# Channel stage: the outer column groups of the Toeplitz tile loaded over 48 of each 64 partitions, on SyncE's queue

## The chip, the cores and the metric

The kernel runs on one core of one Trainium2 chip. The metric is the device time of one execution in microseconds (us), the median of several runs. The time before is 10363.48 us, the median of 3 runs from 10363.17 to 10363.57.

## The reference

Four layers follow each other on an image tensor x of shape (32, 192, 56, 56), each a residual on a group-normalized input (32 groups of 6 channels):

```
x = x + agent_attention(_gn(x))            # layer 0
x = x + bidirectional_wkv_scan(_gn(x))     # layer 1
x = x + shift_and_3x3(_gn(x), offset)      # layer 2
x = x + long_conv(_gn(x), z, W1, W2, W3)   # layer 3
```

Layer 2 moves each channel by its own whole number of rows and columns and applies a separable 3 x 3 kernel of its own. Layer 3 makes a 55 x 55 filter for each channel out of a small network and convolves each 56 x 56 image with it, so that the output row j takes the input rows j-27 to j+27:

```
def _L3_conv_ref(x, z, W1, ..., deltas, shift, bias, distance_map):
...
    xf = jnp.fft.rfft2(x, s)
    kf = jnp.fft.rfft2(k[0], s)
    y = jnp.fft.irfft2(xf * kf[None], s)
    y = y[..., Kh // 2:Kh // 2 + H, Kw // 2:Kw // 2 + W]
    return y + bias * x
```

Layers 2 and 3 work within a channel (and the group of 6 channels for the normalization); the kernel runs them together in its last stage, the channel stage.

## The kernel before, in words

Everything is float32. The program first makes the filters and writes, for every channel, a table `spans` to HBM: for each channel 7 column groups of 128 rows of 84 numbers (42 frequencies, cosine and sine). Then come the attention stage (layer 0), the scan stage (layer 1), which writes its result to HBM as `x2` with a channel's 32 images together, and from about 8243 us to the end the channel stage, `channel_blocks` (L1550). The change touches only this stage.

The channel stage works on one channel at a time, with all 32 images in one tile: the 128 partitions are two halves of 64 (even and odd images), 56 of them image rows. The loop at its end runs c from -1 to 204 and treats three channels in each turn, 6 or 12 channels apart, so that a group of 6 is finished before its mean and spread are needed. In iteration c:

- `load(c + 3)` issues two DMAs on SyncE's queue (SP in the profile), one for each half: 56 rows of 3584 bytes from `x2` into one of ten `x` tiles.
- `norm(c + 2)` normalizes on GpSimd (POOL) with two operations on 128 x 896 (tile `xn`). Every fourth channel, `find_matrices` makes the next shift matrices there.
- `move_rows(c + 1)` shifts and filters along the rows: 8 matmuls into two PSUM banks, two copies on ScalarE (ACT) into `across`.
- `analyse(c - 11)` transforms a centred channel along one axis: matmuls against a table (`ps<-fixed,padded` in the profile), 12 copies on ACT into `y`.
- `move_columns(c)` is the second half of layer 2 (`ps<-cols,across`), added to `x` on VectorE (DVE).
- `synthesise(c - 13)` and `finish` (`ps<-z,fixed`): the inverse transform, added on DVE into `done`, and two DMAs to the output on SP's queue, each of 896 pieces of 224 bytes.
- `convolve(c - 12)`: for each of 42 frequencies a matmul of the spectra `y` with a slice of the Toeplitz tile (`ps<-toep,y`), the product over all input rows at once. ACT moves the result to `turned` in three steps; DVE transposes it for the next turn.
- `load_toeplitz(c - 9)` (L1655 to L1663) loads the Toeplitz tile for the channel that is three turns ahead, into the one of three `toep` tiles that this turn's `convolve` has just read. This is one DMA of 2352 KB on ACT's queue.

The matmuls stand in the program in the order rows, analysis, columns, synthesis, convolution, and on every engine the order of the program is kept (`_InOrder`, L1538), queue issues included. Where instructions of different engines meet, semaphores are put in by the framework. For DMAs of both hardware queues it has eight semaphores, handed out in turn in the order in which its scheduler lists the DMAs; each DMA issue therefore waits until the one handed out eight places earlier has landed.

A `toep` tile is 128 partitions by 56 output rows by 84 numbers. The 128 partitions are the cosine and sine parts of 64 input rows each (56 in use, in reversed order). The 56 output rows are 7 column groups of 8 (`SPAN`); partition p of group q holds 8 consecutive rows, 2688 bytes, that start at row p of the group's 128 rows in `spans`. Rows beyond the reach of the filter are zeros in the table. All constant tiles are cleared once at the stage's start (L1589 to L1596).

Of the kernel before, what the change touches and what calls it, by code (L numbers as in the profile page):

```python
# [30 lines left out]
S = 56  # L31
# [37 lines left out]
HALF = 64  # L69
FREQ = 2 * NF  # L70
LAGS = 2 * S
SPAN = 8
# [1477 lines left out]
def channel_blocks(ctx: ExitStack, tc: tile.TileContext, taps, k, x2, rs2, spans, out):  # L1550
# [8 lines left out]
    nc = tc.nc  # L1559
# [7 lines left out]
    pe, vector, scalar, pool, sync = (_InOrder(tc, e) for e in (nc.tensor, nc.vector, nc.scalar, nc.gpsimd, nc.sync))  # L1567
# [6 lines left out]
    pieces, at = [], 0  # L1574
    for rows, shape in CHANNEL:
        n = int(np.prod(shape))
# [6 lines left out]
    def kept(name, shape, n):  # L1583
        return [cp.tile(shape, F32, name=f"{name}{i}", tag=f"{name}{i}") for i in range(n)]

    xs, padded = kept("x", [128, NI, S], 10), kept("padded", [128, NI, HALF], 8)
    toep, turned = kept("toep", [128, S, FREQ], 3), kept("turned", [128, S, 32], 2)
    across = kept("across", [2 * S, NG, 2, HALF], 2)
    for t in across:  # L1589
        nc.vector.memset(t[:, :, :, S:HALF], 0.0)  # L1590
    for t in xs:
# [63 lines left out]
    def load_toeplitz(c):  # L1655

        if not 0 <= c < C:
            return
        t = toep[c % len(toep)].rearrange("p j f -> p (j f)")
        n = S // SPAN  # L1660
        first = spans[c * n * 128]
        there = bass.AP(first.tensor, first.offset, [[FREQ, 128], [128 * FREQ, n], [1, SPAN * FREQ]])
        scalar.dma_start(out=t.rearrange("p (q f) -> p q f", q=n), in_=there)  # L1663

    def move_rows(c):

# [136 lines left out]
    for c in range(3):  # L1803
        load(c)
        load_toeplitz(c)
        if c < 2:
            norm(c)
    rows, spectra = {}, {}

    def within(c):  # L1810
        return 0 <= c < C

    for c in range(-1, C + LATE + 1):
        m, b, e = c - GROUP, c - LATE, c - LATE - 1
        q = groups[m // GROUP] if within(m) and m % GROUP == 0 else None
# [29 lines left out]
        if within(b):  # L1845
            convolve(b, spectra.pop(b))
            load_toeplitz(b + 3)
# [23 lines left out]
@with_exitstack  # L1871
def all_blocks(ctx: ExitStack, tc: tile.TileContext, a, k, out):
    nc = tc.nc
    NB = out.shape[0]
    dp = ctx.enter_context(tc.tile_pool(name="dram", bufs=1, space=DRAM))

    def scratch(name, shape):
        return dp.tile(shape, F32, name=name, tag=name)

    x1, x2 = scratch("x1", [NB, C, N]), scratch("x2", [C, 2, S, NB // 2, S])  # L1880
    filt, rs2 = scratch("filt", [C, KS * KS]), scratch("rs2", [C, 2, 2, NB // 2])
    lags, taps = scratch("lags", [C, 2, LAGS, FREQ]), scratch("taps", [128, C // 4, 12])
    spans = scratch("spans", [C * (S // SPAN) * 128 + SPAN, FREQ])
    st_a, st_c = scratch("st_a", [128, 2, NB // 2, 9]), scratch("st_c", [2, 64, 2, NB // 2, 9])
    with tc.tile_pool(name="a_r", bufs=1) as rp, tc.tile_pool(name="a_x", bufs=2) as xp:
        ready = _Ready(rp, xp)
        make_filter(tc, a, k, filt, lags, spans, taps, lambda: ready.load(nc, a, k))
        attention(tc, a, ready, x1, st_a, st_c, lambda b: copy_spans(tc, lags, spans, b))
    with tc.tile_pool(name="count", bufs=1) as cp:
        count = cp.tile([1, 1], I32, name="count", tag="count")  # L1890
        scan_pairs(tc, a, k, x1, st_a, st_c, x2, rs2, count)
        n = nc.values_load(count[0:1, 0:1], min_val=0, max_val=128)
        with tc.If(n > 0):
            scan_guarded(tc, a, k, x1, x2, rs2)
    channel_blocks(tc, taps, k, x2, rs2, spans, out)
# [109 lines left out]
```

## Time and profile before

| what | value |
|---|---|
| median of 3 runs | 10363.48 us |
| the profiled execution's own time | 10372.07 us |
| its span (first to last instruction) | 10370.2 us |
| mean granted TensorE clock | 0.962 |
| busy over the whole span: PE / DVE / ACT / POOL | 91% / 88% / 61% / 21% |
| start of the channel stage (first toep load issued) | 8242.9 us |
| first and last convolution matmul | 8348.6 and 10356.6 us |
| toep load: number, size, queue | 192 of 2352.0 KB, ACT |
| x load, channel stage: number, size, queue | 384 of 196.0 KB, SP |
| output store: number, size, queue | 384 of 196.0 KB, SP |

PE, PEld, DVE, ACT, POOL and SP are TensorE's matmuls, its weight loads, VectorE, ScalarE, GpSimd and SyncE; a q behind a name means the queue that issues (ACTq, SPq). L1546 is the helper that records every instruction of the channel stage, so these are told apart by their tiles, written out<-in. A bracket behind a row is the time the engine stood idle before it and what ended that. The granted clock is given as a share of full speed. The share of DMA is the mean over the core's 16 DMA engines and can pass 1 a little, since packets overlap.

### The profile page before, as it was taken

What the parts mean: (1) busy time and instruction counts of PE and PEld (TensorE: products, weight loads), DVE (VectorE), ACT (ScalarE), POOL (GpSimd) and SP (SyncE); (2) the same over time, 40 slices, a digit from 0 to 9 for tenths busy, and PEclk for the clock granted to TensorE, in tenths of its full rate; (3) what the DMA queues carried; (4) which work ended last, traced back from release to release, by engine and by line L of the source; (5) the groups of instructions that cost most, each with busy time, mean ns of one, the idle gap of its engine ahead of it and who ended that gap; (6) DMA issues with size and microseconds to landing.
All of it is one profiled execution on the core that took longest, in us unless ns stands there. A gap on an engine that the chain in (4) does not pass through costs nothing. (4 is left out here: it accounts for less than half of the span.)

```text
span 10370.2 us, 162899 instructions
## 1 busy us (share of the span) xinstructions
PE 9436.8 (91%) x63814; PEld 5816.8 (56%) x63814; DVE 9099.9 (88%) x11284; ACT 6324.4 (61%) x11964; POOL 2223.2 (21%) x1751
## 2 busy tenths in 40 slices
PE   5999999999999999998888888888888799999998
PEld 3555555655565555555333343333334488888886
DVE  5888888888888888887999999999999788888887
ACT  3555555555555555554566666666666567777777
POOL 0000000000000000000333333333333354554442
PEclk9999999999999999998899999999999899999999
DMA  4212221122112211111244444344444489999999
GB/s 129 68 37 66 68 68 44 58 68 68 47 55 68 68 46 29 49 49 43 69 107 101 103 103 105 104 104 101 101 101 101 129 247 303 307 306 304 304 304 278
DMA packets 1111096, 1247.61 MB, mean 120 GB/s; under 512 B 773091, under 2 KB 813440, under 8 KB 1098232
## 3 DMA queue, kind: packets, MB, share of 16 engines
q1 hardware_dynamic: 914284, 746.65, 28.1%
q10 hardware_dynamic: 196036, 490.46, 13.9%
q8 instruction: 506, 8.29, 0.3%
q14 instruction: 270, 2.21, 0.1%
HBM read 916.15 MB, written 306.43 MB: 118 GB/s over the span
## 5 line engine op out<-in xcount | busy, mean ns | idle before, releaser
L649 DVE SCALAR_TENSOR_TENSOR o<-v_a,att_w,o 128x896 f32<-128x896 f32 (+1 forms) x1024 | 1056.8, 1032 | 422.2 <-ACT v_a L623 301.9
L1167 POOL MEMSET f<- 128x2 f32 x48 | 4.5, 99 | 4751.2 <-DMA st_c<-st 4748.8
L1546 DVE STREAM_TRANSPOSE z<-turned 128x1792 f32<-128x1792 f32 x192 | 680.3, 3543 | 211.2 <-ACT turned L1546 211.2
L1546 ACT COPY y<-ps 64x252 f32<-64x252 f32 (+1 forms) x2304 | 784.6, 341 | 89.6 <-PE ps L1546 59.8
L1161 ACT ACTIVATE pq<-pq 128x784 f32<-128x784 f32 x384 | 329.4, 858 | 676.6 <-DVE pq L1157 676.4
L1153 DVE TENSOR_TENSOR_SCAN pq<-decay,f,both 128x784 f32<-128x784 f32 x384 | 695.7, 1841 | 9.1 <-ACT both L1183 9.1
L1157 DVE SCALAR_TENSOR_TENSOR pq<-both,eu,pq 128x1568 f32<-128x1568 f32 x384 | 701.3, 1840 | 2.0 <-POOL f L1156 0.4
L666 ACT ACTIVATE pr<-ps,low 98x896 f32<-98x896 f32 (+1 forms) x384 | 352.3, 918 | 572.7 <-DVE low L664 572.7
L1153 DVE TENSOR_TENSOR_SCAN pq<-decay,b,both 128x784 f32<-128x784 f32 x384 | 694.1, 1839 | 0.0
L921 PE MATMUL ps<-x,weights 128*128 128x392 f32 x1536 | 584.6, 519 | 83.4 <-ACT x L1141 54.2
L649 DVE SCALAR_TENSOR_TENSOR o<-v_c,att_w,o 128x448 f32<-128x448 f32 (+1 forms) x1024 | 638.6, 624 | 4.9
L662 PE MATMUL ps<-xs_a,gk_a 128*98 128x448 f32 (+1 forms) x1536 | 636.8, 495 | 0.0
L776 ACT ACTIVATE pq<-pq 128x1176 f32<-128x1176 f32 (+2 forms) x224 | 241.9, 1080 | 642.5 <-DVE pq L768 620.5
L663 PE MATMUL ps<-xs_c,gk_c 125*98 125x448 f32 (+1 forms) x1536 | 631.3, 492 | 0.0
L1141 ACT ACTIVATE x<-x,nb,rs 128x784 f32<-128x784 f32 x384 | 386.5, 1030 | 337.3 <-DMA x<-x 183.2
L1546 PEld LDWEIGHTS ps<-toep,y 128*32 128x32 f32 x16896 | 500.4, 151 | 160.9 <-issue 76.0
L763 PE MATMUL ps<-gq_a,xs_a 128*128 128x294 f32 (+1 forms) x1600 | 547.0, 425 | 37.7 <-DVE pq L768 33.1
L1546 PE MATMUL ps<-toep,y 128*32 128x112 f32 x16896 | 560.5, 286 | 12.6 <-DVE done L1546 11.1
L1156 POOL COPY b<-pq 128x2 f32<-128x2 f32 x192 | 394.7, 2056 | 660.9 <-DVE pq L1153 567.3
L1546 POOL TENSOR_TENSOR xn<-x,scale 128x896 f32<-128x896 f32 x192 | 329.7, 1717 | 937.4 <-DMA x<-x 670.5
L764 PE MATMUL ps<-gq_c,xs_c 125*128 125x294 f32 (+1 forms) x1600 | 519.9, 413 | 0.0
L1546 ACT ACTIVATE turned<-ps,rs 128x448 f32<-128x448 f32 (+1 forms) x576 | 377.3, 663 | 223.3 <-PE ps L1546 216.0
(360 smaller groups left out, 23488.2 us busy)
## 6 DMA issues: line engine op xcount, KB each, us to landing
toep<-spans ACTq DMA_DIRECT2D x192, 2352.0 KB
x<-x SPq DMA_DIRECT2D x576, 392.0 KB
x<-x SPq DMA_DIRECT2D x896, 196.0 KB
out_x<-done SPq DMA_DIRECT2D x384, 196.0 KB
spans<-lags SPq DMA_DIRECT2D x24, 2352.0 KB
x<-in_x SPq DMA_DIRECT2D x32, 1568.0 KB
x<-x SPq DMA_DIRECT2D x32, 1568.0 KB
gq_c<-once SPq DMA_DIRECT2D x32, 821.1 KB
```

The lines of the kernel that those rows point to most:

```text
L649: nc.vector.scalar_tensor_tensor(dst, tap(i), dww[:, t, i : i + 1], dst, ALU.mult, ALU.add)
L662: mm(ps[P2, h, :n], g[:, cols], xs_a[j][:, px], start=True, stop=False)
L663: mm(ps[P2, h, :n], gk_c[0:KC, 2 * j + h, cols], xs_c[j][0:KC, px], start=False, stop=True)
L666: nc.scalar.activation(pr[:, :, :n], ps[P2, :, :n], AF.Exp, bias=low[:, j, p : p + 1], accum_out=sums[:, j, p : p + 1])
L763: mm(ps[:m, k - q, :HA], xs_a[j][:, px], g, start=True, stop=False)
L764: mm(ps[:m, k - q, :HA], xs_c[j][0:KC, px], gq_c[0:KC, which[k]], start=False, stop=True)
L921: mm(out, aa, srcs[t][h], start=True, stop=False)
L1141: nc.scalar.activation(xs[t], xs[t], AF.Identity, bias=nb1[:, t, s.p : s.p + 1], scale=rs1[:, t, s.p : s.p + 1])
L1153: nc.vector.tensor_tensor_scan(to, decay[:, of(t)].to_broadcast([128, MC]), data, at[:, i : i + 1], ALU.mult, ALU.add)
L1156: nc.gpsimd.tensor_copy(at, z[:, :, last])
L1157: nc.vector.scalar_tensor_tensor(before, both, eu[:, of(t)], before, ALU.mult, ALU.add)
L1546: return lambda *args, **kw: self.tc.keep_in_program_order(do(*args, **kw))
```

## The change

The seven column groups are no longer loaded by one DMA. The middle three (groups 2 to 4) are loaded as before on ACT's queue, now 1008 KB. The outer four are loaded in pairs (groups 0 and 1, groups 5 and 6) by four DMAs on SP's queue, one for each pair and each 64-partition half: 48 partitions of 5376 bytes, 252 KB each. For groups 0 and 1 these are partitions 8 to 55 of the half, read from group 1's rows in `spans`; for groups 5 and 6 partitions 0 to 47, read from group 5's. The 16 partitions of each half that are left out are cleared at the stage's start, by 18 memsets on DVE (for three tiles, two halves and three ranges, 32 partitions by 1344 numbers each). Nothing of the arithmetic changes.

```diff
     across = kept("across", [2 * S, NG, 2, HALF], 2)
+    EDGE = 8
+    for t in toep:
+        for p in (0, HALF):
+            nc.vector.memset(t[p : p + 32, 0 : 2 * SPAN], 0.0)
+            nc.vector.memset(t[p + 32 : p + 64, 0 : 2 * SPAN], 0.0)
+            nc.vector.memset(t[p + 32 : p + 64, 5 * SPAN :], 0.0)
     for t in across:
         nc.vector.memset(t[:, :, :, S:HALF], 0.0)
...
         first = spans[c * n * 128]
-        there = bass.AP(first.tensor, first.offset, [[FREQ, 128], [128 * FREQ, n], [1, SPAN * FREQ]])
-        scalar.dma_start(out=t.rearrange("p (q f) -> p q f", q=n), in_=there)
+        there = bass.AP(
+            first.tensor, first.offset + 2 * 128 * FREQ, [[FREQ, 128], [128 * FREQ, 3], [1, SPAN * FREQ]]
+        )
+        scalar.dma_start(out=t.rearrange("p (q f) -> p q f", q=n)[:, 2:5], in_=there)
+        for q, p, to in ((1, EDGE, 0), (5, 0, 5)):
+            for m in range(2):
+                there = bass.AP(
+                    first.tensor, first.offset + (q * 128 + m * HALF) * FREQ, [[FREQ, S - EDGE], [1, 2 * SPAN * FREQ]]
+                )
+                at = HALF * m + p
+                sync.dma_start(out=t[at : at + S - EDGE, to * SPAN * FREQ : (to + 2) * SPAN * FREQ], in_=there)
```

## The prediction, made before the changed kernel ran

> **What bounds the kernel now.** I read the slices of the span first, then the windows of the channel stage, the list of waits, the DMA queues, and one iteration of the timeline.
>
> ```profile
> PE   5999999999999999998888888888888799999998
> DMA  4212221122112211111244444344444489999999
> ```
>
> From about 8350 us on, PE and the DMA engines are both full. The windows and the queues say how full (columns: time, then each engine's busy time, granted clock, DMA share, GB/s):
>
> ```profile
> 8600.00:10000.00 1400.00, 1375.54 (x19248) 1168.30 (x19248) 1222.22 (x1229) 1064.97 (x2413) 691.26 (x594) 1.00 1.02 304
> ```
>
> ```profile
> q10 hardware_dynamic: 17102, 45.19, 65.1%
> q1 hardware_dynamic: 36831, 15.11, 35.3%
> ```
>
> PE is busy for 98% and DMA for 102% (in the window from 9000 to 9200, 65.1% is ACT's queue, q10: the Toeplitz loads). Which of them is the limit is told by who waits for whom in the same 1400 us:
>
> ```profile
> POOL xn L1546 <- DMA x<-x: 476.9, 84, 13.7
> ...
> ACT turned L1546 <- PE ps L1546: 142.5, 207, 2.0
> ```
>
> No row has PE waiting for a DMA. Only POOL waits for one, the x loads, and one iteration shows why that is free:
>
> ```profile
> 9306.29 1.82 PE L1546 MATMUL ps<-rows,xn 128*112 128x112 f32 x16
> 9306.46 0.37 ACTq L1546 DMA_DIRECT2D toep<-spans  x1
> ...
> 9307.95 2.46 PE L1546 MATMUL ps<-fixed,padded 128*128 128x168 f32 x16
> ...
> 9310.25 1.94 PE L1546 MATMUL ps<-cols,across 112*128 112x112 f32 x16
> ...
> 9312.11 1.73 PE L1546 MATMUL ps<-z,fixed 128*64 128x448 f32 x8
> ...
> 9313.77 2.87 PE L1546 MATMUL ps<-toep,y 128*32 128x112 f32 x88
> ...
> 9315.86 1.69 POOL L1546 TENSOR_TENSOR xn<-x,scale 128x896 f32<-128x896 f32 x1 [7.33 <-DMA x<-x]
> 9316.03 2.52 SPq L1546 DMA_DIRECT2D x<-x  x2
> 9316.57 1.82 PE L1546 MATMUL ps<-rows,xn 128*112 128x112 f32 x16
> ...
> 9317.63 1.69 POOL L1546 TENSOR_TENSOR xn<-xn,scale 128x896 f32<-128x896 f32 x1
> ```
>
> PE runs rows, analysis, columns, synthesis, convolution back to back and starts again after 10.28 us. The xn finished at 9319.3 is read by the rows that start at about 9326.8: 7.5 us in hand. The toep load at 9306.46 is for the convolution three turns later. By the starts of the convolutions in the timeline the common period is 10.26 us; the mean of the 167 periods between 8475.6 and 10247.0 is 10.607, since every sixth turn has the group's mean and spread (11.3 to 12.8) and some lose 0.3 to 1.5 to DVE. So PE sets the pace, with 0.35 us a turn lost on top.
>
> **The change, part by part.**
>
> *Bytes.* Toeplitz falls from 2352 to 1008 + 4 x 252 = 2016 KB, 14%. By the queue's row that is 0.14 x 65.1 = 9 points of DMA share, 1.02 to 0.93. PE never waits for it, so it is worth nothing directly; at most the DVE losses shrink (see the rival).
>
> [...]
>
> *Memsets.* 18 of 32 x 1344. The rows beside them are 128x128 at 165 ns and 128x560 at 525 ns, 0.83 ns an element, so 1.18 us each and 21 us on DVE.
>
> ```profile
> 8244.72 1.12 DVE L1596 MEMSET turned<- 128x560 f32 x2
> ...
> 8270.37 0.62 DVE L1546 TENSOR_TENSOR x<-x,ps 128x448 f32<-128x448 f32 x1 [24.54 <-PE ps L1546]
> ```
>
> DVE's idle 24.5 us hides them; without that cover they would cost 21. The first pieces on SP wait for them, with the x of channels 1 to 3 queued behind. Bounds 0 and 8 us (three pieces of queue), taken: 2.
>
> *Moved to SP, and the semaphores.* This decides. A turn had five DMAs; now it has nine: x, x, out, out, four pieces on SP, and the middle load on ACT. With eight semaphores in turn, every issue waits for the landing of the DMA eight places earlier in the built order. I read that order in the changed program: before, the issue that waits for a Toeplitz load was mostly an output store, two turns after that load. After, the second x half of channel c+3 (which the loop issues at the start of iteration c) waits for the middle load of channel c-9, which ACT issues at the *end* of iteration c. So x(20) waits for toep(8), x(21) for toep(9), for every x from channel 18 to 191. In one iteration of six it is the first half, in one the last piece that stands ahead of both halves. Queued behind it on SP: the next stores, the four pieces, the next first half. Stores and pieces have over a turn of slack (the pieces land some 15 us after their convolution and are read at about 31), x has not: it must be normalized for the rows two turns on.
>
> From the end of iteration c's convolution to the rows of channel c+3, at the start of iteration c+2:
> - to the middle load issued: 0.15 + 0.37 = 0.5 (9306.46 above, next to rows at 9306.29);
> - its landing. By the trace's completion records a 2352 KB load nearly alone (the last turns, after 10250) takes 7.4 to 8.5 us for 15 engines and up to 9.9 for the last, and 12.65 in the median of the full stage. The middle load has 32 fewer packets an engine, at 107 ns (the quicker of q10's packet records) 3.4 us less: 4.2 to 6.5 alone, 9.2 crowded. SP's queue holds 3.7 us of x and stores for a turn (35.3% of 10.5) plus 2.8 of pieces (192 packets at twice the 118 ns that the page gives one of q10's: 13.9% of 16 x 10370 us over 196036; by 16 engines), released together after the previous middle load, so in a turn of 12 us it is nearly drained when the next one starts: 5.5;
> - wait seen, x half issued: 0.5;
> - its landing: 2.4 to 2.9 us in a quiet stretch (8324 us), 7.3 in the median of the full stage behind stores. It is now the first in a drained queue: 2.6;
> - norm: 2 x 1.69 and the hand-overs, 3.5, and 0.1 to PE.
>
> Together 12.7; the iterations with the first half (+0.8) and the piece (+1.5, a piece and two issues ahead) add 2.3/6 = 0.4: **D = 13.1**. Only one iteration, c+1, lies between, and PE's work from rows to the end of the convolution is 10.28 - 0.1 = 10.15, plus 0.2 for the group turns. The end of iteration c+2 is then the end of c plus D plus 10.35, so two periods are 23.45 and one is 11.73. The stall comes mostly on every second turn (2.9 us), and after a long idle PE is slow:
>
> ```profile
> 8305.30 2.76 PE L1546 MATMUL ps<-rows,xn 128*112 128x112 f32 x16 [4.29 <-POOL xn L1546]
> ```
>
> 2.76 for 1.82 here and 2.68 for 1.94 in the columns behind it: 1.7 us after 4.3 of idle, but nothing after the 1.7 us gaps of the last turns. For 2.9 I take 0.5 in each second turn: +0.25. **Period 12.0**, 1.39 more than 10.607, over the 174 channels from 18 to 191: 242 us. With the 2 of the start, +244. On the profiled span of 10370.2 that is 10,614; the median lies 6.7 under that span, so **10,608**.
>
> Ends: all low (4.2 and 2.4, no extras, no slow PE) D is 11.1 and the period (11.1 + 10.35)/2 = 10.73, +21: 10,385. All high (9.2 and 7.3) D is 21.1, period 15.7: +890, 11,250.
>
> **The rivals.**
> - *The queues stay crowded.* x and the middle load share engines with late pieces and stores: 7.5 and 5.0 in the sum, D 17.5, period 13.9 + 0.25, +620: 10,980. For it: DMA is still 93% full by the bytes. Against: a longer period empties it.
> - [...] The x lands earlier with less traffic; POOL's xn then runs clear of DVE's centring, which takes 2.3 us beside POOL and 1.1 alone, and the period falls to 10.26 plus the group turns' 0.17. (10.607 - 10.43) x 174 = 31 less: 10,333. It decides from D under 10.15, that is, landings of 5.2 us together where the quiet rows give 6.6.
> - *No change.* The wait is met before x is wanted: 10,363. Same threshold against it, at D = 10.5.
> - *The pieces come too late for the convolution*: needs 16 us more lateness than worked out. Left at 2%.
>
> **How the numbers follow.** Forecast 80%, crowded queues 10%, late pieces 2%, faster 5%, no change 3%. That gives slower 0.92, same 0.03, faster 0.05; within 0.2% (21 us) the measurement can't tell. The forecast's own span goes from a D of 11.6 (10,430) to 15.2 (period 13.0 with the slow PE, 10,780); to leave no more than 2 in 10 outside with the crowded case I go to 10,430 to 10,830.
>
> **What would show it.** Right: PE idle before `ps<-rows,xn`, ended by POOL xn, and POOL xn ended by DMA x, in nearly every second turn; SP's x issues lasting until the middle load has landed; convolution starts alternating near 10.3 and 13; DMA share well under 0.9; the last 12 turns at 8.7 us as before. Wrong: a period of 10.3 to 10.6 with no idle before rows (the wait is met), PE waiting for toep, or the time lost at the stage's start, where the memsets are.

## The result, and the profile after

The changed kernel takes 11,090.47 us in the median of 4 runs (11,084.22 to 11,093.22), against 10,363.33 us for the kernel before on the same chip: a ratio of 1.0703, 95% interval 1.0684 to 1.0721, 727 us longer. The forecast was 10,608 us, with 10,830 as its upper end: the sign and the mechanism came out, the size did not. The profiled execution is one of 11,084.22 us, with a span of 11,082.4.

The slices of the span, first (busy tenths of 40 slices; PEclk is the granted clock in tenths):

```profile
PE   6999999999999999988888888888877877887777
PEclk8999999999999999998999999999988998989888
DMA  4222111222222111113444434444447888888888
```

Nothing has changed up to the channel stage, the last quarter. There PE falls from 9 to between 7 and 8, DMA from 9 to 8, and the granted clock from 9 to between 8 and 9: both are now idle at times. The window from 8600 to 10,000 us has the numbers (time, then busy time of PE, its weight loads, DVE, ACT and POOL, the granted clock, the share of DMA, GB/s):

```profile
8600.00:10000.00 1400.00, 1108.44 (x14063) 961.71 (x14063) 908.65 (x901) 787.98 (x1774) 488.73 (x432) 0.90 0.86 199
```

PE is busy for 79% of this time instead of 98%. DMA moves 199 GB/s instead of 304, but its engines are still 86% taken. The queues, in the window from 9000 to 9200 us as before (packets, MB, share of 16 engines), show that the two don't fit together:

```profile
q1 hardware_dynamic: 29851, 24.72, 59.4%
q10 hardware_dynamic: 5554, 14.36, 25.8%
```

Before, these two queues moved 60.3 MB in 100.4% of the engines' time; now they move 39.1 MB in 85.2%. A MB takes 31% more engine time. The list of waits between 8600 and 10,000 us says what the stall is (what waits and for what; us in total, times, the longest):

```profile
PE ps L1546 <- POOL xn L1546: 291.5, 87, 8.1
...
POOL xn L1546 <- DMA x<-x: 711.6, 76, 14.2
...
SPq L1546 <- DMA toep<-spans: 826.0, 106, 11.2
```

PE waits for the norm, the norm for x, and SyncE's queue, which issues x, for a Toeplitz load. That is the predicted chain, and the trace has it in every turn: of the 118 middle loads issued between 8480 and 10,180 us, 80 are waited for by the second x half, 19 by the first and 19 by the last piece, as forecast, and each of the 118 waiting transfers has been issued within 1 us of the load's landing. One turn in the timeline, of the form in which the piece waits (start, duration, instruction, idle before it):

```profile
9319.59 11.57 SPq L1546 DMA_DIRECT2D toep<-spans  x4
...
9320.98 0.37 ACTq L1546 DMA_DIRECT2D toep<-spans  x1
...
9331.20 0.84 SPq L1546 DMA_DIRECT2D x<-x  x2
...
9336.25 1.69 POOL L1546 TENSOR_TENSOR xn<-x,scale 128x896 f32<-128x896 f32 x1 [13.07 <-DMA x<-x]
9338.02 1.69 POOL L1546 TENSOR_TENSOR xn<-xn,scale 128x896 f32<-128x896 f32 x1
...
9339.76 3.06 PEld L1546 LDWEIGHTS ps<-rows,xn 128*112 128x112 f32 x16 [4.81 <-POOL xn L1546]
9339.76 3.33 PE L1546 MATMUL ps<-rows,xn 128*112 128x112 f32 x16 [4.57 <-POOL xn L1546]
```

ACT issues the middle load at 9320.98. By the trace's completion records it has landed at 9330.84, and at 9330.85 SyncE gets its fourth piece out (the end of the group of four that stands from 9319.59), and the two x halves behind it. PE idles for 4.57 us, and the rows then take 3.33 us instead of 1.82.

All of the loss lies in this stage, which starts 13.8 us earlier in this trace than before (its first Toeplitz load is issued at 8229.1 us). The mean of the 167 periods between convolutions that the prediction used (before: 10.607 us) is 14.545, which makes 167 x 3.94 = 658 us; the first twelve turns take 38 us more than before and the last thirteen 24, and the first convolution starts 6.6 us earlier, 7 us later after the stage's start than before. Together that is 713, against 712.2 between the two spans.

### The profile page after: what moved, and what is told of

Read it like the earlier page. It is cut to its first block, busy times and chain, and to the rows that moved or that the text cites. A ratio compares the mean times of both kernels' runs of the same rounds, so it can differ in the third digit from the quotient of the medians.

```text
span 11082.4 us, 164604 instructions
## 1 busy us (share of the span) xinstructions
PE 9618.5 (87%) x63814; PEld 6006.6 (54%) x63814; DVE 9144.4 (83%) x11302; ACT 6333.3 (57%) x11964; POOL 2190.3 (20%) x1751
## 5 line engine op out<-in xcount | busy, mean ns | idle before, releaser
L1546 PE MATMUL ps<-rows,xn 128*112 128x112 f32 x3072 | 487.7, 332 | 585.4 <-POOL xn L1546 559.4
L1546 DVE TENSOR_TENSOR x<-x,ps 128x448 f32<-128x448 f32 x384 | 237.6, 620 | 713.8 <-issue 443.1
L1546 PEld LDWEIGHTS ps<-rows,xn 128*112 128x112 f32 x3072 | 445.3, 238 | 629.1 <-POOL xn L1546 626.3
L1546 ACT COPY across<-ps 112x448 f32<-112x448 f32 x384 | 204.0, 532 | 868.9 <-PE ps L1546 748.2
```

What stands on the lines that cost most here:

```text
L1546: return lambda *args, **kw: self.tc.keep_in_program_order(do(*args, **kw))
```

## The experiments

Two measures are used throughout. The *period* is the mean of the same 167 periods. The *packet time of a turn* is the share of DMA, summed over all queues between 8480 and 10,180 us, times the period: the engine time that the transfers of one turn take. It is 10.8 us before and 12.5 after, although a turn has 14% fewer bytes of Toeplitz rows. A packet's time is not a fixed price: the same middle load's packets take 131 ns in the mean in e4 and 150 in the changed kernel, where more is under way. Each ratio is to runs of the kernel before beside the same set, whose medians go from 10,363 to 10,378 us, so differences between sets are good to some 15 us.

| kernel | Toeplitz loads of a turn | DMAs | median us | ratio to before, 95% interval | period us | packet time us |
|---|---|---|---|---|---|---|
| before | one, ACT | 5 | 10,363 | 1 | 10.61 | 10.8 |
| changed | middle ACT, 4 x 48 SP | 9 | 11,090 | 1.0703 (1.0684 to 1.0721) | 14.55 | 12.5 |
| e1 | middle SP, 4 x 48 SP | 9 | 10,693 | 1.0302 (1.0282 to 1.0322) | 12.32 | 12.4 |
| e2 | five groups ACT, 2 x 48 SP | 8 | 10,710 | 1.0315 (1.0290 to 1.0340) | 12.46 | 11.7 |
| e3 | one ACT, 4 tiny SP | 9 | 10,515 | 1.0130 (1.0108 to 1.0151) | 11.35 | 10.6 |
| e4 | middle ACT | 5 | 10,331 | 0.9953 (0.9934 to 0.9973) | 10.35 | 6.7 |
| e5 | as changed, x on GpSimd | 9 | 10,740 | 1.0357 (1.0339 to 1.0374) | 12.50 | 12.4 |
| e6 | as e2, scales on GpSimd | 8 | 10,557 | 1.0153 (1.0086 to 1.0220) | 11.76 | 12.0 |
| e7 | as changed, x a turn earlier | 9 | 10,997 | 1.0603 (1.0577 to 1.0628) | 13.97 | 12.4 |
| e8 | as changed, middle of 336 KB | 9 | 10,729 | 1.0341 (1.0324 to 1.0358) | 12.50 | 10.3 |
| e9 | middle and 2 x 128, all SP | 7 | 10,434 | 1.0062 (1.0045 to 1.0079) | 10.93 | 10.9 |
| e10 | as e1, half the bytes a piece | 9 | 10,330 | 0.9959 (0.9944 to 0.9974) | 10.35 | 9.5 |
| e11 | as e1, pieces of 128 x 2016 bytes | 9 | 10,330 | 0.9965 (0.9955 to 0.9975) | 10.34 | 9.8 |
| e12 | middle ACT, 2 x 128 SP | 7 | 10,618 | 1.0239 (1.0222 to 1.0256) | 12.15 | 10.8 |
| e13 | middle SP, 4 x 64, each in one half | 9 | 10,935 | 1.0534 (1.0518 to 1.0550) | 13.54 | 13.6 |
| e14 | middle SP, 4 x 64, across the middle | 9 | 10,445 | 1.0065 (1.0049 to 1.0080) | 10.94 | 10.9 |
| e15 | one ACT, memsets added | 5 | 10,371 | 0.9993 (0.9983 to 1.0002) | 10.65 | 10.9 |
| e16 | one of 120 partitions, ACT | 5 | 11,154 | 1.0743 (1.0728 to 1.0758) | 14.75 | 14.5 |

### First question: is it the wait for the middle load?

**e1: the middle load on SyncE's queue.**

```diff
-        scalar.dma_start(out=t.rearrange("p (q f) -> p q f", q=n)[:, 2:5], in_=there)
+        sync.dma_start(out=t.rearrange("p (q f) -> p q f", q=n)[:, 2:5], in_=there)
```

> As the changed kernel, but the middle Toeplitz load is issued by SyncE instead of ScalarE, so all nine DMAs of a turn stand on one queue; their number, bytes and shapes are unchanged. Theory (SyncE's transfers wait for a semaphore that the middle load issued on the other queue at the end of the turn still holds): now every such wait is on a DMA issued earlier on the same queue, so no x load waits for the end of the current turn; the gap before the first norm waiting on x disappears and the time is 10,330 to 10,420 us. Rival (the narrower pieces and their added bytes and packets crowd the transfers that x needs, whoever issues): at least as slow as the changed kernel, 11,090 us or more, since SyncE's queue is now longer.

Neither of the two. 10,693 us gives back 398 of the 727, so the wait across the queues is more than half of the loss; 330 stay, which the theory had no place for. The queues between 8480 and 10,180 us show why:

```profile
q1 hardware_dynamic: 363616, 394.79, 99.4%
```

Here the DMA engines are full, at 234 GB/s where the kernel before has them full at 305. The packet time of a turn, 12.4 us, is the period: without the wait across the queues the kernel is bound by its transfers, and these got more expensive. (SyncE's queue still waits 529 us for Toeplitz loads in these 1700 us, 996 in the changed kernel, but now for loads issued earlier on itself, and the engines do not run dry meanwhile.) This split the question in two.

**e2: pieces for one side only, eight DMAs a turn.**

```diff
-            there = bass.AP(first.tensor, first.offset + 2 * 128 * FREQ, [[FREQ, 128], [128 * FREQ, 3], ...
+            there = bass.AP(first.tensor, first.offset, [[FREQ, 128], [128 * FREQ, 5], [1, SPAN * FREQ]])
...
-        for q, p, to in ((1, EDGE, 0), (5, 0, 5)):
+        for q, p, to in ((5, 0, 5),):
...
+        there = bass.AP(first.tensor, first.offset, [[FREQ, 48], [1, 4]])
+        sync.dma_start(out=tiny[c % len(toep)][0:48], in_=there)
```

> Only the last two column groups come as two pieces on SyncE; groups 0 to 4 stay in one load of 128 partitions on ScalarE's queue, and SyncE issues one more load of 48 partitions by 4 numbers into a tile of its own, which nothing reads. A turn has 8 DMAs, as many as there are semaphores, so most transfers wait for the one of the same kind a turn before, and the middle load of the current turn's end is waited for by none that x needs. Theory: 10,340 to 10,400 us although half of the pieces are kept. Rival (pieces cost by their packets or bytes): about half of the loss remains, 10,700 us.

The time is the rival's, but the turns are the theory's: five of six mostly take 10.25 to 12 us, and each sixth, the one with the loads of scales, about 20. The timeline of such a turn:

```profile
9342.64 15.51 SPq L1546 DMA_DIRECT2D scale<-rs  x2
...
9348.16 0.37 ACTq L1546 DMA_DIRECT2D toep<-spans  x1
...
9358.25 1.21 SPq L1546 DMA_DIRECT2D out_x<-done  x2
...
9369.47 1.69 POOL L1546 TENSOR_TENSOR xn<-x,scale 128x896 f32<-128x896 f32 x1 [13.65 <-DMA x<-x]
```

The two extra loads shift the count of eight, and the second load of scales waits for ACT's load of 9348.16, which lands at 9357.69; it goes out at 9357.70. Stores, pieces and x stand behind it. Where the count has no such wait, the turn is short, with the same pieces around it.

**e6: the same, with the scales off SyncE's queue.**

```diff
-            sync.dma_start(
+            pool.dma_start(
                 out=scales[n][HALF * s : HALF * s + HALF], in_=rs2[n * GROUP, s].partition_broadcast(HALF)
```

> As the kernel with pieces for the last two column groups only and eight DMAs a turn, but the two small loads of scales, which every sixth turn adds, are issued by GpSimd. In the profile of that kernel five turns of six took 10.25 to 11.5 us and each sixth about 20, in which SyncE's second load of scales was issued at the moment at which the middle load of the same turn had landed; with these loads gone from SyncE, the built order has no wait for a middle load of the same or a later turn. Theory: the sixth turn falls to about 10.8 us, 32 times 9 less: 10,380 to 10,450 us. Rival (pieces crowd, and the sixth turn is long for the work that it has beside): 10,650 us or more.

Between the two: 10,557 us (10,453 to 10,607). The long sixth turns of some 20 us are gone, as expected, but now the middle half of all turns takes 11.2 to 12.1. The engines are full, with a packet time of 12.0 us and a period of 11.76. And there is a wait that the expectation did not have, on ScalarE (8480 to 10,180 us):

```profile
ACT across L1546 <- DMA toep<-spans: 391.9, 97, 5.8
```

With eight DMAs a turn ACT's Toeplitz load waits for ACT's own load of the turn before. All 144 loads of this stretch go out within 0.15 us of that landing, so they follow each other one at a time: 11.78 us from an issue to its landing, 0.02 to the next issue, which is the period. ACT's own work stands behind the waiting issue, since its order is kept. So e6 is no proof that two narrow pieces alone set its pace.

**e5: x issued by GpSimd.**

```diff
-            sync.dma_start(out=x[HALF * s : HALF * s + S], in_=x2[c, s])
+            pool.dma_start(out=x[HALF * s : HALF * s + S], in_=x2[c, s])
```

> As the changed kernel, but the two x loads of a turn are issued by GpSimd, whose transfers have eight semaphores of their own; pieces, middle load, stores, bytes and shapes are unchanged. In the built order x then waits only for x loads of four turns before, while a piece or a store waits for the middle load of the next turn's end, with a turn to spare. Theory (what costs is that x stands behind a wait for the middle load): the gap before the first norm goes, 10,340 to 10,450 us, the upper end if issuing on GpSimd takes time from the norm. Rival (narrow pieces and middle load crowd x and each other, whatever the wait): x lands late here too, 10,700 us or more.

The first part came true: PE has no wait for the norm left (0.0 us before the rows, 351 in the changed kernel between 8480 and 10,180 us). The time did not; it is the rival's, but not for the rival's reason. The wait is still on SyncE's queue, and now the out stores stand behind it (DVE's and PE's waits in the same window):

```profile
DVE done L1546 <- DMA out_x<-done: 386.2, 108, 9.5
...
PE ps L1546 <- DVE z L1546: 102.2, 62, 6.9
PE ps L1546 <- DMA toep<-spans: 53.8, 30, 3.4
```

The result tile has two buffers; a store that comes late holds up DVE, and DVE holds up PE. With a packet time of 12.4 us and a period of 12.50 there would be nothing to gain beyond e1 anyway.

**e7: x loaded four turns ahead.**

```diff
-    xs, padded = kept("x", [128, NI, S], 10), ...
+    xs, padded = kept("x", [128, NI, S], 11), ...
-            load(c + 3)
+            load(c + 4)
```

> As the changed kernel, but x is loaded four turns ahead instead of three, into 11 buffers instead of 10; nine DMAs a turn, the same queues. The late wait stays, in the built order mostly on the first out store of a turn, which stands before the x loads of the next on SyncE's queue and waits for the middle load of that next turn's end. Theory: the loop from the convolution's end to the rows of the same x is the same 17.6 + 11.5 us, but spans three turns instead of two: 9.7 us, below TensorE's own 10.3 to 10.6, so most of the loss goes: 10,370 to 10,600 us, the upper end if the late out store holds up the tile that the next result is written to. Rival (crowding): little changes, over 10,900 us.

A miss: only 93 us come back. PE's wait for the norm falls from 351 us to 95, but DVE waits 442 us for out stores. Moving the stalled load forward left the queue stalled (SyncE's queue still waits 875 us for Toeplitz loads in these 1700 us, 996 in the changed kernel), and the next transfer on it paid.

**e12: full rows in two wide loads, middle load on ACT.**

```diff
-        for q, p, to in ((1, EDGE, 0), (5, 0, 5)):
...
+        for q, to in ((0, 0), (5, 5)):
+            there = bass.AP(first.tensor, first.offset + q * 128 * FREQ, [[FREQ, 128], [128 * FREQ, 2], ...
+            sync.dma_start(out=t.rearrange("p (q f) -> p q f", q=n)[:, to : to + 2], in_=there)
```

> As the changed kernel, middle load on ScalarE's queue, but the outer groups come on SyncE's as two loads of 128 partitions with the full rows; nothing is zeroed. Seven DMAs a turn; in the built order x waits for earlier transfers of SyncE's own queue, and an out store for the middle load of the turn before. Theory: neither the late wait nor the narrow pieces are left, so the kernel is back at 10,360 to 10,480 us. Rival (splitting a load over two queues costs by itself): 10,550 us or more.

Also a miss: the time is the rival's, but the trace has the reason in a wait across the queues once more. In the expectation a store that waits for the previous turn's middle load was taken as harmless. The timeline says it is not:

```profile
9317.87 0.37 ACTq L1546 DMA_DIRECT2D toep<-spans  x1
9318.32 10.44 SPq L1546 DMA_DIRECT2D out_x<-done  x2
...
9328.85 1.13 SPq L1546 DMA_DIRECT2D toep<-spans  x2
9330.03 1.22 SPq L1546 DMA_DIRECT2D x<-x  x2
```

The load of 9317.87 lands at 9328.40, 10.2 us after its issue has ended, and the second store goes out at 9328.42. A whole turn of SyncE's queue is lost, and the x behind it is late. Against e9, which differs in the queue of the middle load alone, this costs 184 us.

### Second question: how long is the chain?

**e8: a middle load of one column group.**

```diff
-            first.tensor, first.offset + 2 * 128 * FREQ, [[FREQ, 128], [128 * FREQ, 3], [1, SPAN * FREQ]]
+            first.tensor, first.offset + 3 * 128 * FREQ, [[FREQ, 128], [128 * FREQ, 1], [1, SPAN * FREQ]]
```

> As the changed kernel with the same waits, but the middle load carries column group 3 alone, 336 KB instead of 1008; groups 2 and 4 of the Toeplitz rows stay zero, so their share of the result is left out. It measures what the middle load's landing is worth. Theory: the landing falls from 9.5 us by 2 to 4, the chain from convolution to rows with it, the period by half of that, 1 to 2 us of 14.5: 10,720 to 10,900 us. Rival (the landing is a fixed latency and the rest is what counts): 11,050 to 11,090 us.

As expected, near the lower end of the range. The chain in parts, from the trace's start and completion records for channels 30 to 185:

| part, us | prediction | changed kernel | e8 |
|---|---|---|---|
| convolution's end to middle load issued | 0.5 | 0.54 | 0.49 |
| its landing | 5.5 | 9.54 | 6.42 |
| x half issued after that | 0.5 | 0.55 | 0.56 |
| x landing | 2.6 | 3.16 | 2.84 |
| norm, hand-overs, to PE | 3.6 | 3.80 | 3.80 |
| other forms of the wait | 0.4 | - | - |
| D | 13.1 | 17.59 | 14.12 |
| W, rows to the convolution's end | 10.35 | 11.53 | 10.95 |
| (D + W)/2 | 11.73 | 14.56 | 12.53 |
| measured period | | 14.55 | 12.50 |

D and W together are two periods by their definition, so the last two rows agree of themselves. What the table shows is which part differs from the forecast: the steps around the two landings took what was forecast, to 0.2 us, and the landing of the middle load took 4.0 us more. The packet records say what fills it. In its 9.5 us, in the mean over the 118 loads, the engines spend 3.6 us on its own packets, 3.5 on pieces and 1.3 on stores and x.

**e4: no pieces at all.**

```diff
-        for q, p, to in ((1, EDGE, 0), (5, 0, 5)):
+        for q, p, to in ():
```

> The changed kernel without the four pieces; the outer four column groups of the Toeplitz rows stay zero, so their share of the result is left out. Five DMAs a turn, 1008 KB of rows instead of 2352. Theory: the x loads wait for a middle load of two turns before, so the gap goes; TensorE's own work sets the period as before: 10,330 to 10,363 us. If bytes alone had bounded the kernel before, it would fall well below 10,330.

10,331 us, as expected: the middle load on ACT does no harm where a turn has five DMAs. Its landing, 7.5 us in the mean although no piece is under way, is on nobody's path.

**e3: the kernel before with four tiny loads.**

```diff
         scalar.dma_start(out=t.rearrange("p (q f) -> p q f", q=n), in_=there)
+        for i in range(4):
+            there = bass.AP(first.tensor, first.offset + i * 128 * FREQ, [[FREQ, 48], [1, 4]])
+            sync.dma_start(out=tiny[c % len(toep)][0:48, i], in_=there)
```

> The kernel before with four more loads of 48 partitions by 4 numbers a turn, issued by SyncE after the Toeplitz load into a tile that nothing reads: nine DMAs a turn, as in the changed kernel, nearly no bytes moved. In the built order their small size lets the x loads be handed the semaphore of an earlier DMA than in the changed kernel: it is the tiny loads themselves that wait for the Toeplitz load of the turn before, which has landed long since. Theory (which wait falls on x decides, not the count): 10,365 to 10,400 us. Rival (nine issues a turn on the queues are the cost): 10,900 us or more.

A miss by 115 us, and not the rival either. PE waits 2 us for the norm in 1700, so x is in time, but SyncE's queue waits 389 us for stores (4 before) and 132 for Toeplitz loads. PE's waits for DVE rise from 26 to 95 us in the same stretch. The trace has the way there, through ScalarE (ACT's and DVE's waits between 8480 and 10,180 us):

```profile
ACT across L1546 <- DMA tiny<-spans: 102.1, 29, 6.2
ACT across L1546 <- DMA x<-x: 68.5, 20, 5.7
ACT across L1546 <- DMA toep<-spans: 33.4, 7, 5.6
...
DVE sums L1546 <- ACT sq L1546: 160.3, 93, 4.6
```

Of the 150 Toeplitz loads on ACT's queue 126 go out within 0.15 us of the landing that their semaphore waits for, and ACT is idle for 352 us before these (before: 29 of 160, and 64 us). ACT's copies stand behind the waiting issue, so DVE waits 160 us for ACT's squares (23 before), and PE for DVE. No run takes this wait away by itself, so how much of the loss of some 140 us it makes is not measured. The kernel before has a trace of it, in the list that the prediction read as having POOL alone wait for a DMA:

```profile
ACT across L1546 <- DMA toep<-spans: 16.5, 6, 4.2
```

### Third question: why are the pieces expensive?

The packet records of the trace have the time of each packet. These are the means between 8480 and 10,180 us:

| transfer | kernel | partitions | bytes a packet | mean ns |
|---|---|---|---|---|
| whole load | before | 128 | 2688 | 124 |
| middle load | changed / e1 | 128 | 2688 | 150 / 138 |
| piece | changed / e1 | 48, one half | 5376 | 390 / 381 |
| wide outer and middle loads | e9 | 128 | 2688 | 122 |
| wide piece | e11 | 128 | 2016 | 87 |
| piece | e13 | 64, one half | 5376 | 366 |
| piece | e14 | 64, across the middle | 5376 | 223 |
| whole load | e16 | 120 | 2688 | 196 |

**e9: the outer groups in two wide loads, all on SyncE.** The edit is that of e12 on top of e1.

> All Toeplitz loads on SyncE's queue as in the kernel with the middle load moved there, but the outer groups come as two loads of 128 partitions with the full rows (two packets of 2688 bytes a partition) instead of four pieces of 48 partitions; 2352 KB a turn again, seven DMAs. The profiles so far say that the pieces' packets of 5376 bytes took 381 to 395 ns each, where twice the middle load's 2688 would be 214 to 300, and that the DMA engines were 98 to 100% busy where all transfers stood on SyncE, with 12.33 us of packet time a turn against 10.83 before. Theory (a transfer into 48 partitions of one half of the tile's partitions is slow, whoever issues it): the wide packets take 107 to 130 ns, the packet time of a turn falls to 10.6 to 11.0 us, the time to 10,360 to 10,480. Rival (SyncE's one queue, its number of transfers and their order, bounds that kernel): 10,570 us or more.

As expected: 10,434 us, with 17% more bytes of Toeplitz rows than e1 and 259 us less. The queue:

```profile
q1 hardware_dynamic: 455634, 499.04, 98.6%
```

The engines are as full as in e1, but move 499 MB in these 1700 us instead of 395. The 62 us that are left against the kernel before are the price of three loads on SyncE's queue instead of one on ACT's: PE waits 80 us for the norm.

**e11: the pieces' bytes on 128 partitions.**

```diff
-        for q, p, to in ((1, EDGE, 0), (5, 0, 5)):
...
+        for q in (0, 1, 5, 6):
+            there = bass.AP(first.tensor, first.offset + q * 128 * FREQ, [[FREQ, 128], [1, 504]])
+            sync.dma_start(out=t[:, q * SPAN * FREQ : q * SPAN * FREQ + 504], in_=there)
```

> As the kernel with all loads on SyncE, nine DMAs a turn and the same 252 KB in each piece, but a piece is 128 partitions of 504 numbers (2016 bytes) instead of 48 of 1344: the first three quarters of each outer group; the last quarter stays zero, so its share of the result is left out. Bytes, number, queue and order of transfers are those of that kernel; only the partitions differ. Theory: packets of 2016 bytes take 80 to 100 ns, the packet time of a turn 10.3 to 10.6 us, the time 10,340 to 10,450. Rival (number and order of SyncE's transfers): unchanged, 10,690 us.

Nine transfers a turn, one queue, 252 KB a piece, everything as in e1 but the shape: 10,330 us instead of 10,693, just under the expected range. Neither number nor order of SyncE's transfers bounds e1; the shape of the pieces does.

```profile
q1 hardware_dynamic: 486170, 471.40, 93.5%
```

**e10: pieces of 48 partitions with half the bytes.**

```diff
-                    first.tensor, ..., [[FREQ, S - EDGE], [1, 2 * SPAN * FREQ]]
+                    first.tensor, ..., [[FREQ, S - EDGE], [1, 672]]
```

> As the kernel with all loads on SyncE, but each of the four pieces of 48 partitions carries 672 numbers, 2688 bytes a partition, instead of 5376; the rest of the outer columns stays zero, so its share of the result is left out. It tells the packet's size from its place. Theory (48 partitions of one half are slow): the 2688-byte packets of the pieces take about half of the 381 ns, 180 to 210, while the middle load's of the same size take 107 to 140; time 10,330 to 10,430 us, since the packet time of a turn falls to about 10.1. Rival (packets over some size are slow): 107 to 130 ns for both.

The time is as expected, 10,330 us. Pieces and middle load now have packets of one size, a third of them pieces, with a mean of 151 ns. With 131 ns (e4) to 138 (e1) for the middle load's, the pieces' come to 3 x 151 - 2 x 131 = 191 or 3 x 151 - 2 x 138 = 177 ns: half of the 381, so the packet's size is not the reason.

**e13 and e14: the same pieces in one half, and across the middle.**

```diff
         for k, q in enumerate((0, 5)):
-            for p, to in ((0, t[:, q * SPAN * FREQ : (q + 2) * SPAN * FREQ]), (64, spare[:, k])):
+            for p, to in ((32, t[:, q * SPAN * FREQ : (q + 2) * SPAN * FREQ]), (32, spare[:, k])):
                 there = bass.AP(first.tensor, first.offset + (q * 128 + p) * FREQ, [[FREQ, 64], [1, 2 * SPAN * FREQ]])
                 sync.dma_start(out=to[p : p + 64], in_=there)
```

> As the kernel with all loads on SyncE, but the four pieces are 64 partitions of 5376 bytes: for each outer pair of groups one into partitions 0 to 63 of the Toeplitz tile, and one into partitions 64 to 127 of a tile that nothing reads; the rest of the outer groups stays zero, so its share of the result is left out. Theory (a transfer into one half of the partitions goes at half the rate): packets of 5376 bytes take 400 to 480 ns, 256 of them by 16 engines are 6.4 to 7.7 us a turn, the packet time of a turn 14 to 15 us, the time 10,950 to 11,150. Rival (48 partitions are slow because they are few or don't divide well): 64 are quicker, 214 to 300 ns, 10,400 to 10,600 us.

> The same, and the same bytes, packets and tiles, but all four pieces go to partitions 32 to 95, half of them on each side of the middle. Theory (half of the partitions, by sides): packets of 5376 bytes take 210 to 260 ns, 3.4 to 4.2 us a turn, the packet time of a turn 10.6 to 11.3 us, the time 10,370 to 10,520. Rival (few partitions, or packets of 5376 bytes, are slow wherever they lie): 400 ns and 10,950 us or more, as in the other kernel of this pair.

These two differ in nothing but the partitions. e13's queue and then e14's:

```profile
q1 hardware_dynamic: 338059, 401.26, 100.0%
```

```profile
q1 hardware_dynamic: 420668, 499.66, 98.6%
```

Same number, size and queue of the transfers; 366 ns a packet against 223, 10,935 us against 10,445. 64 partitions are not slow as such here; 64 that lie in one half are. In e13 packets are somewhat quicker than the 400 to 480 expected, and the time 15 us under the range.

**e15: the memsets alone**, added to the kernel before.

> The kernel before with the 18 memsets of the Toeplitz tiles, each of whose results the next load overwrites; nothing else is changed. Theory: they lie in VectorE's idle time at the start of the stage, 0 to 3 us. Rival: 18 times 1.18 us on the path, 21 us.

No difference that can be told: 0.9993 (0.9983 to 1.0002).

**e16: the kernel before with a load of 120 partitions.**

```diff
-        there = bass.AP(first.tensor, first.offset, [[FREQ, 128], [128 * FREQ, n], [1, SPAN * FREQ]])
-        scalar.dma_start(out=t.rearrange("p (q f) -> p q f", q=n), in_=there)
+        there = bass.AP(first.tensor, first.offset, [[FREQ, 120], [128 * FREQ, n], [1, SPAN * FREQ]])
+        scalar.dma_start(out=t[0:120].rearrange("p (q f) -> p q f", q=n), in_=there)
```

> The kernel before, but the one Toeplitz load of a turn takes 120 partitions instead of 128 (the last eight hold no image row and are zeroed once); still one load on ScalarE's queue and five DMAs a turn, 2205 KB instead of 2352. Theory: its packet time falls by 6%, from 6.97 to 6.5 us a turn, and as 252 KB less in wide packets (the nine-transfer kernel with 128 partitions) or 1344 KB less (the middle load alone) were both worth 40 to 47 us, some of these come back: 10,330 to 10,360. Rival (120 partitions are split over fewer engines, which are then as long as before): 10,363 to 10,375 us.

Neither, and by far: 11,154 us. Of a load's 16 completion records one now comes 0.2 to 0.4 us after the issue, where before the first came after 7.7 us, so that 15 are left for the data; and its packets take 196 ns instead of 124. The packet time of a turn, 14.5 us, nearly fills the period of 14.75: 6% fewer bytes made this the slowest kernel of the study.

## Why the prediction was wrong in size

The wait across the queues and the bill for the pieces make up the loss. In this table the columns differ in the queue of the middle load alone, the rows in the outer loads (their form, and with it their number and bytes; e11 and e13 against e14 show that the form is what counts):

| median us | middle load on ACT | middle load on SyncE |
|---|---|---|
| outer groups 4 x 48 partitions | 11,090 (changed) | 10,693 (e1) |
| outer groups 2 x 128 partitions | 10,618 (e12) | 10,434 (e9) |

From before to the changed kernel: 62 to 71 us for three loads on one queue (e9), 259 for narrow pieces (e1), 398 for the middle load on the other queue. The parts depend on each other: with wide outer loads the other queue costs 184 (e12 against e9).

Point by point:

- *Bytes: 0.14 x 65.1 = 9 points of DMA share less, worth nothing.* Wrong sign for what a turn's transfers cost: their packet time rose from 10.8 to 12.5 us, and the share fell to 0.86 only because the turn became longer still. The prediction's own slices showed DMA at 9 to the end and the window a share of 1.02; it read this as free because PE waited for no DMA. Full engines that PE does not wait for yet were a bound all the same: at a packet time of 12.4, e1 runs at 12.32, and at 13.6, e13 runs at 13.54.
- *The pieces' packets at twice the 118 ns of q10's*, 2.8 us a turn, and with them the landing of the middle load, 5.5 us: **this is the step that failed.** The pieces' packets took 390 ns, and 192 of them over 16 engines are 4.7 us. They were scaled from a row for 128 partitions by bytes alone. The queue was to be "nearly drained" when the middle load starts; instead pieces take 3.5 us of its landing, which was 9.54 in the mean. x landed in 3.16 instead of 2.6. D became 17.59 instead of 13.1. The pieces are not the whole error: without any the load still lands in 7.5 us (e4), so 5.5 was low in any case, and no run makes the pieces alone cheaper while the middle load stays on ACT. That the landing sets the period is shown by e8: it is 3.12 us shorter there (6.42), half of which is 1.56 of the 2.05 us by which the period falls (12.50).
- *Slow PE after idle: +0.25 a turn.* Mis-sized too, as the stall was larger: W was 11.53 instead of 10.35, half of which is 0.59. The rows took 331 ns a matmul in the mean, 267 before. The stall was to fall mostly on every second turn; PE waited for the norm 107 times in the 117 turns between 8480 and 10,180 us. The two terms make (4.49 + 1.18)/2 - 0.25 = 2.58 of the 2.55 us by which the period of 12.0 fell short.
- *The mechanism* was right: which transfer waits for which, the order on SyncE's queue, the norm on the path, and the halving. The rival with crowded queues (7.5 us for the middle load, 10,980) was the nearest, given 1 in 10; against it the prediction argued that a longer period empties the queues, but every turn needs 12.5 us of packets, and at a period of 14.55 the engines were still taken for 86%.
- *The memsets* alone cost nothing that can be told (e15), as forecast. What the pieces' wait for them costs (0 to 8 us, taken 2) no run shows by itself; from the stage's start to the first convolution the changed kernel takes 7 us longer. *The low end* is mis-added: its parts make a D of 11.2, not 11.1, which gives 10,393. *The last turns at 8.7 us* was wrong: they ran at 8.75 to 13.69, 24 us in all, since the wait goes on to the end; and the first turns lost 38.
- *Faster, no change, late pieces*: none came. Between 8600 and 10,000 us PE waited for nothing but the norm.

What the prediction did not weigh is where the pieces land: packets into one half took 64% longer than the same across the middle (e13 against e14: 366 ns against 223), and the pieces of 48 lie in one half each. With two loads of 128 partitions in place of the four pieces, on the same queue, 259 us come back (e9 against e1). No run shows why packets into one half are slower, nor why those of e16's load of 120 partitions took 196 ns against 124.

## What to carry to other kernels

Price a new transfer from a row with the same partitions, not by its bytes alone: here 14% fewer bytes of rows made a turn's transfers 16% dearer, because they went to one half of the partitions at a time (390 ns a packet of 5376 bytes; 223 across the middle in e14). The kernel before had a nearer row, the x loads into 56 partitions of one half: 192 ns for 3584 bytes, which makes 288 for 5376; still short of the 390 measured, but nearer than 236. Where transfers of two queues share semaphores, ask for each issue which landing it waits for and what stands behind it; moving the load that is late only handed the wait to the next one in the queue (e7, e12, and e5, where full engines bound the kernel as well), and keeping the loads on one queue took it off (SyncE's queue waits 996 us for Toeplitz loads in the changed kernel, 529 in e1, 35 in e9). Look at the issuing engine too: what waits on ACT's queue holds up ACT's own work (352 us of idle time in 1700 in e3, 508 in e6). And when DMA is full beside a busy engine, count its packet time a turn as a second bound, with its own sum (12.4 us in e1, at a period of 12.32).

## What the runs showed of the hardware

- 64 partitions in one half of the 128: 366 ns for a packet of 5376 bytes; the same across the middle: 223 (206 in the median), about twice the 107 of a quick packet of 2688.
- 120 partitions instead of 128: one of a load's 16 completions 0.2 to 0.4 us after the issue, where the first came after 7.7 us before, and 196 ns a packet instead of 124; 11,154 us instead of 10,377.
- A wait for a load on the other queue ends within 0.02 us of its landing (9330.84 and 9330.85; 9357.69 and 9357.70; 9328.40 and 9328.42), and holds up all that is behind it, in the changed kernel for up to 11.2 us. On ACT's queue it holds up ACT's own work: 508 us of idle time in 1700 in e6, before 144 loads.
- After 2.45 us of idle PE took 2.88 us for 16 matmuls of the rows, after 4.57 us 3.33, and 1.82 without idle time; the analysis behind the first of these took 3.09 instead of 2.46. These are single turns: in the changed kernel between 8480 and 10,180 us the rows took 1.82 to 3.33 us after 2 to 3 us of idle (2.37 in the mean of 17 turns), and 3.17 in the mean of 29 after 4 to 6 us.
